# A depthwise convolution spread over four engines and issued a chunk ahead, in a gated-scan kernel

## Chip, cores and metric

One core of one Trainium2 chip; all data is fp32. The metric is device microseconds of one execution. The engines are called PE (TensorE, matmuls), DVE (VectorE), ACT (ScalarE) and POOL (GpSimd); PEld is PE's weight load. SBUF and PSUM are the two on-chip memories.

## The reference, cut to what matters

For each of 4 images of 128 channels and 96x96 pixels, in four scan directions:

```python
t = grouped_1x1(groupnorm(x), in_proj_w, in_proj_b)      # 128 -> 512 channels
u, gate = t[:, :256], t[:, 256:]
u = depthwise_conv(silu(u), dw_w)                        # 5 taps along the scan order
s = ssm_in_w @ u                                         # 32 channels, like a, bb, cc
a = DMIN + (DMAX - DMIN) * sigmoid(ssm_delta_w @ u + ssm_delta_b)
bb, cc = tanh(ssm_b_w @ u + ssm_b_b), tanh(ssm_c_w @ u + ssm_c_b)
h = a * h_prev + bb * s                                  # the scan, along 9216 pixels
u = u + ssm_out_w @ (cc * h + ssm_d * s)
y = out_proj(mix(u * sigmoid(gate)))                     # then fused over the directions
out = x + fuse_w @ y
```

## The kernel before

A *phase* is one image in one pixel order; silu(in_proj(x)) lies whole in SBUF (`sil`), and two *passes*, one for each direction, read it. There are 16 passes. A pass has 18 chunks of 480 pixels and two of 288 (19.3 full ones). In a second pass the front part of the next phase (in_proj and silu) runs too. The 256 channels are two halves of 128. The parts that the change touches:

```python
    def front(ph, c):                      # groupnorm and silu(in_proj) of one chunk
        nc.vector.tensor_scalar(xn, xn, norm[:, 0:1], norm[:, 1:2], ALU.subtract, ALU.mult)
        ...                                # two matmuls pts[j] = w_in . xn, then for each half j
            nc.scalar.activation(sg[:, :n], pts[j][:, :n], AF.Sigmoid, bias=b_in[:, j : j + 1])
            nc.vector.scalar_tensor_tensor(sil[...], pts[j][:, :n], b_in[...], sg[:, :n], ALU.add, ALU.mult)

    def conv_and_gate(st):
        for k, w in taps:                  # half 0: five matmuls with diagonal weights, in PSUM
            nc.tensor.matmul(pu[:, :n], diag[:, w, :], sil[:, 0, bass.ds(o + k, n)], start=..., stop=...)
        for k, w in taps:                  # half 1: one tap on ACT, four on DVE
            if k == 0:
                nc.scalar.activation(u[:, 1, :n], src, AF.Copy, scale=coef)
            else:
                nc.vector.scalar_tensor_tensor(u[:, 1, :n], src, coef, u[:, 1, :n], ALU.mult, ALU.add)
        nc.scalar.copy(u[:, 0, :n], pu[:, :n])
        ...                                # gates: two matmuls pg[j], two sigmoids into gv

    def scan(st):
        ...                                # pp = w_proj . u; tanh, sigmoid, tanh on 32 rows each
        ...                                # POOL: a scaled and clipped; DVE: b*s, scan, c*h, + d*s -> z

    def ssm_out(st):
        ...                                # pu += w_so . z (half 0); pz = w_so . z (half 1)
        nc.vector.tensor_mul(gv[:, 0, :n], pu[:, :n], gv[:, 0, :n])
        nc.vector.tensor_add(u[:, 1, :n], pz[:, :n], u[:, 1, :n])
        nc.vector.tensor_mul(gv[:, 1, :n], u[:, 1, :n], gv[:, 1, :n])

    for n, st in enumerate(steps):         # steps: all chunks of all passes
        conv_and_gate(st)
        if prev is not None:
            ssm_out(prev)
        ...                                # front() of the next phase in second passes
        scan(st)
        if prev is not None:
            accumulate(prev)               # py = w_fin . gv (PE), acc += py (DVE)
        prev = st
```

The instructions are not issued quite in this order: a scheduler in the build reorders them, engine by engine.

## Time and profile before

| | before |
|---|---|
| median of 4 runs, us (range) | 3689.91 (3685.10 to 3701.43) |
| PE / DVE / ACT / POOL busy | 96% / 80% / 43% / 11% |
| mean granted PE clock | 0.938 |
| a full chunk, first pass / second pass | 10.5 us / 11.4 and 12.5 us |
| time at half clock, from the trace's clock records | 455 of 3636 us |

The granted clock of PE over the span, in tenths:

```profile
PEclk8899999999999999999999999999999999999999
```

A 9 is 90% or more.

### The profile page before, as it was taken

To read this page: it belongs to the slowest core of one execution; us is meant where nothing else is said; L and a number is where in the kernel's file an instruction comes from. 1 tells how busy PE (TensorE), PEld (TensorE's weight loads), DVE (VectorE), ACT (ScalarE), POOL (GpSimd) and SP (SyncE) were. 2 spreads that over 40 slices of the span, in tenths; PEclk is the share of its full clock that TensorE was granted. 3 is DMA by queue.
4 is the path that set the end of the run, shared out by engine and by line. 5 is a ranking of instruction groups with operands and counts; after the bars stand their busy time and mean duration, and the time that the engine had idled before them with its cause. 6 is when DMAs were issued, how large, how long until landed. Compare 5 with 4: busy or idle time off the path is not lost.

```text
span 3681.5 us, 27637 instructions
## 1 busy us (share of the span) xinstructions
PE 3543.3 (96%) x9032; PEld 1550.5 (42%) x9032; DVE 2937.6 (80%) x4442; ACT 1572.0 (43%) x2572; POOL 393.2 (11%) x653
## 2 busy tenths in 40 slices
PE   7999999999999999999999999999999999999999
PEld 3334444444443444444443444444444344444444
DVE  7788887788877888778887788777887778877777
ACT  3334444444443444444443444444444444444443
POOL 0011111111111111111111011111111111111111
PEclk8899999999999999999999999999999999999999
DMA  4210000002100000001210000000121000000000
GB/s 145 82 37 12 19 22 0 0 30 65 59 3 0 17 19 17 0 0 46 65 45 0 0 20 22 11 0 3 59 62 32 0 4 21 22 6 0 3 24 25
DMA packets 56625, 92.14 MB, mean 25 GB/s; under 512 B 7296, under 2 KB 56352, under 8 KB 56480
## 3 DMA queue, kind: packets, MB, share of 16 engines
q1 hardware_dynamic: 54720, 89.68, 8.0%
q8 instruction: 70, 1.15, 0.1%
q10 hardware_dynamic: 1760, 0.70, 0.1%
q14 instruction: 75, 0.61, 0.1%
HBM read 71.48 MB, written 18.87 MB: 25 GB/s over the span
## 4 chain that ended last, share of the span: by engine, by line
DVE 46%; PE 41%; issue 6%; ACT 4%; DMA 2%; POOL 0%; ACTq 0%; DVEq 0%; POOLq 0%
DVE u L262 12%; PE pp L288 8%; PE pc L325 8%; PE pc L249 8%; DVE h L309 8%; PE py L340 6%; PE pz L329 6%; DVE z L319 5%; DVE tb L303 4%; DVE z L318 4%; DVE gv L332 3%; PE pu L225 3%; DVE u L331 3%; DVE sil L232 3%; ACT u L260 2%
## 5 line engine op out<-in xcount | busy, mean ns | idle before, releaser
L249 PE MATMUL pc<-sil,diag 128*128 128x480 f32 (+1 forms) x3200 | 1299.5, 552 | 0.0
L262 DVE SCALAR_TENSOR_TENSOR u<-sil,w_dw,u 128x480 f32<-128x480 f32 (+1 forms) x1280 | 889.0, 695 | 135.4 <-ACT u L260 124.0
L249 PEld LDWEIGHTS pc<-sil,diag 128*128 128x128 f32 x3200 | 610.7, 191 | 643.3 <-issue 624.7
L288 PE MATMUL pp<-u,w_proj 128*128 128x480 f32 (+1 forms) x1280 | 705.2, 680 | 3.1 <-DVE u L262 2.0
L265 ACT COPY u<-pc 128x480 f32<-128x480 f32 (+1 forms) x320 | 173.8, 543 | 1074.9 <-PE pc L249 1074.8
L340 PE MATMUL py<-gv,w_fin 128*128 128x480 f32 (+1 forms) x1280 | 614.2, 605 | 0.9
L301 POOL TENSOR_SCALAR a<-a 32x480 f32<-32x480 f32 (+1 forms) x320 | 189.8, 593 | 3252.3 <-ACT a L295 3252.3
L330 DVE TENSOR_TENSOR gv<-pc,gv 128x480 f32<-128x480 f32 (+1 forms) x320 | 203.8, 637 | 343.5 <-PE pc L325 337.1
L275 ACT ACTIVATE gv<-pg,b_in 128x480 f32<-128x480 f32 (+1 forms) x640 | 379.2, 642 | 143.8 <-PE pg L271 133.4
L325 PE MATMUL pc<-z,w_so 32*128 32x480 f32 (+1 forms) x640 | 332.6, 599 | 101.8 <-DVE z L319 100.5
L340 PEld LDWEIGHTS py<-gv,w_fin 128*128 128x128 f32 x1280 | 282.6, 222 | 331.4 <-issue 234.6
L288 PEld LDWEIGHTS pp<-u,w_proj 128*128 128x128 f32 x1280 | 244.3, 212 | 390.2 <-issue 273.8
L260 ACT ACTIVATE u<-sil,w_dw 128x480 f32<-128x480 f32 (+1 forms) x320 | 216.8, 678 | 404.7 <-DVE gv L332 398.0
L309 DVE TENSOR_TENSOR_SCAN h<-a,h,tb 32x480 f32<-32x480 f32 (+1 forms) x304 | 354.7, 1167 | 1.1
L271 PE MATMUL pg<-xn,w_in 32*128 32x480 f32 (+1 forms) x1280 | 345.5, 600 | 0.6 <-ACT gv L275 0.6
L229 ACT ACTIVATE sg<-pu,b_in 128x480 f32<-128x480 f32 (+1 forms) x320 | 201.7, 638 | 274.8 <-PE pu L225 274.7
L329 PE MATMUL pz<-z,w_so 32*128 32x480 f32 (+1 forms) x640 | 301.1, 550 | 0.0
L225 PE MATMUL pu<-xn,w_in 32*128 32x480 f32 (+1 forms) x640 | 264.2, 632 | 9.1 <-DVE sil L232 7.7
L293 ACT ACTIVATE tb<-pp,b_proj 32x480 f32<-32x480 f32 (+1 forms) x320 | 204.0, 637 | 150.8 <-PE pp L288 145.1
L303 DVE TENSOR_TENSOR tb<-pp,tb 32x480 f32<-32x480 f32 (+1 forms) x320 | 198.9, 621 | 70.3 <-ACT z L299 67.3
L232 DVE SCALAR_TENSOR_TENSOR sil<-pu,b_in,sg 128x480 f32<-128x480 f32 (+1 forms) x320 | 219.0, 691 | 24.9 <-ACT sg L229 23.5
L331 DVE TENSOR_TENSOR u<-pz,u 128x480 f32<-128x480 f32 (+1 forms) x320 | 203.9, 637 | 43.7 <-PE pz L329 2.6
(54 smaller groups left out, 2122.3 us busy)
## 6 DMA issues: line engine op xcount, KB each, us to landing
xn<-in_xv SPq DMA_DIRECT2D x72, 240.0 KB, 2.6
acc<-in_xh SPq DMA_DIRECT2D x72, 240.0 KB, 2.8
xn<-in_xh SPq DMA_DIRECT2D x72, 240.0 KB, 2.6
out<-res SPq DMA_DIRECT2D x72, 240.0 KB, 2.0
xs<-in_xh SPq DMA_DIRECT2D x54, 240.0 KB, 2.6
xn<-in_xv SPq DMA_DIRECT2D x8, 144.0 KB, 2.4
acc<-in_xh SPq DMA_DIRECT2D x8, 144.0 KB, 2.4
xn<-in_xh SPq DMA_DIRECT2D x8, 144.0 KB, 2.1
```

The costliest lines, as they stand in the source:

```text
L225: nc.tensor.matmul(pt[:, :n], w_in[q, :], xn[q, span(c)], start=True, stop=True)
L232: nc.vector.scalar_tensor_tensor(sil[:, j, bass.ds(PAD + STARTS[c] * WW, n)], pts[j][:, :n], b_in[:, j : j + 1], sg[:, :n], ALU.add, ALU.mult,
L249: nc.tensor.matmul(pu[:, :n], diag[:, w, :], sil[:, 0, bass.ds(o + k, n)], start=(k == 0), stop=(k == K - 1),)
L262: nc.vector.scalar_tensor_tensor(u[:, 1, :n], src, coef, u[:, 1, :n], ALU.mult, ALU.add)
L271: nc.tensor.matmul(pg[:, :n], w_in[q, :], xn[q, span(c)], start=True, stop=True)
L275: nc.scalar.activation(gv[:, j, :n], pgs[j][:, :n], AF.Sigmoid, bias=b_in[:, 2 + j : 3 + j])
L288: nc.tensor.matmul(pp[:, :n], w_proj[:, j, :], u[:, j, :n], start=(j == 1), stop=(j == 0))
L303: nc.vector.tensor_mul(tb[:, :n], s, tb[:, :n])
L309: nc.vector.tensor_tensor_scan(dirn(h), dirn(a), dirn(tb), 0.0 if st["first"] else carry[0], ALU.mult, ALU.add,)
L325: nc.tensor.matmul(pu[:, :n], w_so[:, 0:P], z[:, :n], start=False, stop=True, skip_group_check=True)
L329: nc.tensor.matmul(pz[:, :n], w_so[:, P:HID], z[:, :n], start=True, stop=True)
L340: nc.tensor.matmul(py[:, :n], w_fin[:, d, j, :], gv[:, j, :n], start=(j == 0), stop=(j == 1))
```

## The change

The intent: PE is the bound, so the convolution is taken off it. Half 0 keeps two taps on PE, and DVE adds three. Half 1 moves to ACT (five scaled copies) and POOL (four adds). It is issued a chunk ahead of its use. Sigmoids become tanh(x/2) with their factors folded into weights; silu is one ACT function; groupnorm is folded into `w_in` and the biases, once an image; the last two DVE steps work on both halves at once, 960 columns.

```diff
+PE_TAPS = (1, 2)
 ...
     def front(ph, c):
-        nc.vector.tensor_scalar(xn[:, span(c)], ...)              # groupnorm
-            nc.scalar.activation(sg[:, :n], ..., AF.Sigmoid, ...)
-            nc.vector.scalar_tensor_tensor(sil[...], ...)
+            nc.scalar.activation(sil[...], pts[j][:, :n], AF.Silu, bias=bn[:, j : j + 1])
 ...
+    def conv(st):
+        u = wk.tile([P, 2, CW], F32, tag="u", bufs=3, name=f"u_{id_}")
+        for k in range(K):                                        # half 1: ACT and POOL
+            src, coef, _ = tap(1, k)
+            t = u[:, 1, :n]
+            if k:
+                t = wk.tile([P, CW], F32, tag="tmp", bufs=3, name=f"tmp_{id_}_{k}")[:, :n]
+            nc.scalar.activation(t, src, AF.Copy, scale=coef)
+            if k:
+                nc.gpsimd.tensor_add(u[:, 1, :n], u[:, 1, :n], t)
+        for i, k in enumerate(PE_TAPS):                           # half 0: PE, then DVE
+            nc.tensor.matmul(pu[:, :n], diag[:, w, :], src, start=..., stop=...)
+        part = pu[:, :n]
+        for k in range(K):
+            if k not in PE_TAPS:
+                nc.vector.scalar_tensor_tensor(u[:, 0, :n], src, coef, part, ALU.mult, ALU.add)
+                part = u[:, 0, :n]
 ...
     def scan(st):                      # one tanh on 96 rows for three calls on 32
+        nc.scalar.activation(t[: 3 * MH, :n], pp[: 3 * MH, :n], AF.Tanh, bias=b_proj[:, 0:1])
+        nc.vector.tensor_mul(bs[qa, :n], s, t[qb, :n])            # then scan, z as before
 ...
     def ssm_out(st):
+        nc.vector.tensor_add(pz[:, :, :n], pz[:, :, :n], u[:, :, :n])
+        nc.vector.scalar_tensor_tensor(gv[:, :, :n], gv[:, :, :n], 1.0, pz[:, :, :n], ALU.add, ALU.mult)
 ...
+    conv(steps[0])
     for n, st in enumerate(steps):
+        scan(st)
+        gates(st)
         if prev is not None:
             ssm_out(prev)
         ...                            # front() of the next phase
+        if n + 1 < len(steps):
+            conv(steps[n + 1])
         if prev is not None:
             accumulate(prev)
```

## The prediction

> **What bounds the kernel now.** I read the page's busy table, then timelines of a steady stretch of each kind of pass, then the groups of instructions with shapes kept apart, then how long POOL's instructions took.
>
> ```profile
> PE 3543.3 (96%) x9032; PEld 1550.5 (42%) x9032; DVE 2937.6 (80%) x4442; ACT 1572.0 (43%) x2572; POOL 393.2 (11%) x653
> ```
>
> PE is busy 96% of the span, DVE 80%, POOL hardly at all. Busy PE alone proves little, so this is PE's timeline over one chunk of a first pass (start, us, count at the right):
>
> ```profile
> 1500.27 1.88 PE L288 MATMUL pp<-u,w_proj 128*128 128x480 f32 x4
> 1501.98 1.77 PE L340 MATMUL py<-gv,w_fin 128*128 128x480 f32 x4
> 1503.59 4.19 PE L249 MATMUL pc<-sil,diag 128*128 128x480 f32 x10
> 1507.71 1.07 PE L271 MATMUL pg<-xn,w_in 32*128 32x480 f32 x4
> 1508.96 1.07 PE L325 MATMUL pc<-z,w_so 32*128 32x480 f32 x2 [0.18 <-DVE z L319]
> 1509.87 0.96 PE L329 MATMUL pz<-z,w_so 32*128 32x480 f32 x2
> 1510.77 0.67 PE L288 MATMUL pp<-u,w_proj 128*128 128x480 f32 x1
> ```
>
> The chunk takes 1510.77 - 1500.27 = 10.50 us. A matmul is two instructions, each 0.41 us from start to start (4.12 us for the ten of the convolution). The two gate matmuls, on different rows of the array, run side by side: four instructions in about 0.85 us. Streaming is 22 x 0.41 + 0.85 = 9.9 us of the 10.5; the rest is a wait for z. So **PE's rate** bounds a first pass. In a second pass the front part of the next phase adds two more matmuls and three DVE operations; there the start of L330 goes from 1740.96 to 1752.40 to 1764.95, so 11.4 and 12.5 us a chunk, the longer one with a projection (pp) that took 3.3 instead of 1.7 us. The windows view gives a granted clock of 0.97 in the first pass 569 to 781 and 0.93 in the second pass 781 to 1012. Of the convolution, PE does 5 of 5 taps for half the channels, 4.1 us of every chunk: the largest single item of the bound.
>
> The durations that I use for the new kernel stand in these groups (count, then busy, mean ns):
>
> ```profile
> L262 DVE SCALAR_TENSOR_TENSOR u<-sil,w_dw,u 128x480 f32<-128x480 f32 x1152 | 822.9, 715 | 129.9 <-ACT u L260 120.0
> L309 DVE TENSOR_TENSOR_SCAN h<-a,h,tb 32x480 f32<-32x480 f32 x280 | 335.6, 1198 | 0.7
> L319 DVE SCALAR_TENSOR_TENSOR z<-pp,d_sb,z 32x480 f32<-32x480 f32 x288 | 203.0, 705 | 9.7
> L331 DVE TENSOR_TENSOR u<-pz,u 128x480 f32<-128x480 f32 x288 | 189.3, 657 | 42.0 <-PE pz L329 1.5
> L303 DVE TENSOR_TENSOR tb<-pp,tb 32x480 f32<-32x480 f32 x288 | 184.8, 642 | 62.4 <-ACT z L299 59.8 <-PE py L340 2.5
> L318 DVE TENSOR_TENSOR z<-z,h 32x480 f32<-32x480 f32 x288 | 184.4, 640 | 0.8
> L345 DVE TENSOR_TENSOR acc<-py,acc 128x480 f32<-128x480 f32 x144 | 152.7, 1061 | 37.3 <-PE py L340 37.3
> ```
>
> Last, DVE and POOL already disturb each other. These are the two engines at one place:
>
> ```profile
> 2327.98 1.83 DVE L262 SCALAR_TENSOR_TENSOR u<-sil,w_dw,u 128x480 f32<-128x480 f32 x2
> ...
> 2328.72 0.58 POOL L301 TENSOR_SCALAR a<-a 32x480 f32<-32x480 f32 x1 [10.45 <-ACT a L295]
> 2329.38 0.86 POOL L302 TENSOR_SCALAR a<-a 32x480 f32<-32x480 f32 x1
> ```
>
> Two convolution taps on DVE took 1.83 us where two elsewhere take 1.46, and the second POOL operation took 0.86 where its median is 0.58.
>
> [...] The trace has eight loads of 1.28 us in all, around the square root. [...]
>
> **The change, part by part, for a full chunk (480 columns).**
> PE: the convolution goes from ten instructions to four, -6 x 0.41 = -2.5 us. Nothing else of PE changes in number. A first pass needs 9.9 - 2.5 = 7.4 us, a second pass 8.2 us (another 0.85).
> ACT: five tap scalings in place of one (0.69 us for the first, then one every 0.60: 3.1 us), one tanh on 96 rows for three on 32 (0.66 for 2.0), gates 1.21, no PSUM copy: 5.0 us; in a second pass two silu add 1.25, so 6.2 us. Not a bound.
> POOL: four adds of 128x480 with two inputs. [...]
> DVE: three taps 3 x 0.715 = 2.15; bs 0.64; scan 1.20; z product 0.64; z sum 0.70; [...] accumulate 1.06 in V order, 0.68 in H order, mean 0.87; statistics in 60 of 320 chunks, 0.1. Sum 8.7 us of durations. In the timeline neighbours without dependence start 0.08 us before the end of the one before, so occupancy is about 8.4. The front part no longer needs DVE (normalising 0.52, two silu products 1.42: 1.9 us saved in every second pass).
> So with no interference DVE is the bound at 8.4 us, above PE at 7.4 to 8.2.
>
> **Interference.** Four DVE operations a chunk have two SBUF inputs: scan, z product, and two of the three taps (the first reads PSUM): 1.20 + 0.64 + 1.43 = 3.3 us. [...] 8.4 + 1.3 = 9.7; I take 9.7 us a chunk, in both kinds of pass.
>
> **The sum.** There are 16 passes of 18 full and two short chunks, 19.3 full ones each. Before, first passes take 212 us for 10.5 x 19.3 = 203, so 9 us at the pass's ends and in slow-clock chunks; I keep 7. The head is 36 us to the first front part, as before; the 20 front parts of the first phase then took some 75 us in front of or between the first chunks, now about 20 x 1.25 = 25 (ACT). Tail 8. 36 + 25 + 8 + 16 x (19.3 x 9.7 + 7) = 69 + 16 x 194 = 3176. The pass-end and front terms partly overlap with work that the scheduler can pull in, so I round down to **3150 us**, 15% under 3689.
>
> **Rivals.** (a) *DVE at its own rate, waits hidden*: if POOL's adds fall in DVE's PSUM operations (5 us of them a chunk), the chunk is 8.5 to 9.0 us and the time 2800 to 2950. For it: the order of DVE's instructions in the trace is not the text's order, taps are already pulled into gaps. [...] (b) *A latency loop*: pp waits for both halves of u; then tanh 0.66, POOL's two steps 1.3, scan 1.2, two z steps 1.35, outputs 2.4, taps 2.2, pp again 1.9. If each engine ran strictly in the order of the text this ring is 11 us, 12 and more with blocked taps, and the time 3500 to 3800: no gain. [...] Against: the convolution is issued a chunk ahead and u has three buffers, so the taps need not lie in the ring. (c) *PE again*, at a lower clock: 8.2/0.93 = 8.8 us in a second pass; under my 9.7, so it only shows if interference is small. [...]
>
> **Range and chances.** 8.5 us a chunk gives about 2810, 10.7 about 3490; I put the range there. Faster needs under 3615, a chunk of 11.1 us[...]. Faster 0.90, within 2% 0.06, slower 0.04.
>
> **What would show it.** Right: PE's busy share falls to about 80% or less and DVE's rises to 90% or more; [...] taps of the first half show a mean well over 0.715 us; first and second passes alike in length; eight table loads still. Wrong: taps at 0.72 us and DVE idle waiting for ACT or POOL (then b); [...] PE still over 90% (then c).

Some of its numbers need their source. DVE's 8.7 us hold 1.16 us for the output sum over both halves and 1.21 for the gating over both. A straight line through the sizes of the one-half sum in the trace of the kernel before, 657 ns at 480 columns (L331) and 455 at 288, gives the same 1.16 us at 960; the 1.21 is that plus the 0.05 by which L319 (705 ns) is longer than L331. These are estimates from two sizes. A two-input add on POOL occurs nowhere in that trace, so no trace showed its length, and the 1.3 us of interference, which rests on that length, was the author's estimate. That DVE and POOL lengthen each other is in the trace: of DVE's taps at 480 columns (L262) the 334 that overlap a POOL step on a take 751 ns on average, the 818 others 700; the POOL steps take 663 ns beside a tap or a z product (347) and 580 elsewhere (229).

## The result, and the profile after

The changed kernel is **slower by 15.8%**: 4274.43 us median of 4 runs (4272.09 to 4277.90) beside 3689.91. Both give the right result. The ratio is 1.1575, with a 95% interval of 1.1553 to 1.1597. A ratio here is the mean time of one kernel's runs over that of the other's runs of the same rounds, so not quite the ratio of the medians.

First the page's busy line and clock row of the changed kernel:

```profile
PE 3665.2 (86%) x7120; PEld 1333.0 (31%) x7120; DVE 3018.6 (71%) x3340; ACT 1801.6 (42%) x2895; POOL 2089.5 (49%) x1936
...
PEclk9887878877878787777787788777778788886777
```

No engine is near its rate. The remarkable thing is PE: it has 21% fewer matmuls than before (7120 for 9032) and is busy *longer* (3665 for 3543 us). The clock row says why: it stands at 7 and 8. By the clock records in the trace PE ran 1791 of 4156 us at half clock, where it was 455 of 3636 before.

The groups of instructions, shapes apart (count, then busy us and mean ns, then the idle time of that engine just before them and what ended it):

```profile
L275 POOL TENSOR_TENSOR u<-u,tmp 128x480 f32<-128x480 f32 x1152 | 1581.8, 1373 | 1054.1 <-ACT u L273 933.1 <-ACT tmp L273 51.7
...
L291 DVE SCALAR_TENSOR_TENSOR u<-sil,w_dw,u 128x480 f32<-128x480 f32 x576 | 568.5, 987 | 11.6
...
L365 DVE TENSOR_TENSOR pz<-pz,u 128x960 f32<-128x960 f32 x288 | 335.6, 1165 | 214.7 <-PE pz L362 198.9 <-PE pu L247 13.0
L366 DVE SCALAR_TENSOR_TENSOR gv<-gv,pz 128x960 f32<-128x960 f32 x288 | 332.2, 1154 | 8.7
L353 DVE TENSOR_TENSOR t<-t,h 32x480 f32<-32x480 f32 x288 | 322.5, 1120 | 9.2
```

The taps with two SBUF inputs take 987 ns on average where the same form took 715 before, and the z product (L353) 1120 where it was 640. Both are blocked by POOL's adds: at 480 columns the 325 of these taps that overlap an add take 1199 ns on average, the other 251 take 713; the 207 z products beside an add 1303, the other 81 652. The tap with a PSUM input takes 714 and 713 (worked out from the trace's records). The two double-width operations cost 1165 and 1154 ns, near the estimates of 1.16 and 1.21 us. So durations are about as foreseen; the idle time is not. The waits, longest first, show it:

```profile
ACT tmp L273 <- POOL u L275: 1127.0, 1090, 2.7
POOL u L275 <- ACT u L273: 1015.4, 303, 8.5
...
PEld pp L324 <- DVE u L291: 490.9, 244, 4.8
ACT u L273 <- DVE pz L365: 483.2, 198, 4.5
DVE bs L337 <- ACT t L329: 459.9, 188, 10.6
...
PE pp L324 <- DVE u L291: 295.1, 166, 4.0
```

ACT waits for POOL, POOL for ACT, ACT for DVE, DVE for ACT. And the projection (pp) waits for the last tap on DVE: its weight load did so 244 times, in 320 chunks, where it waited for a tap 6 times in the kernel before. PE's timeline of one stretch (the bracket at the right is idle time before the instruction and what ended it):

```profile
1482.28 1.07 PE L306 MATMUL pg<-xn,wn 32*128 32x480 f32 x4
1485.72 1.93 PE L362 MATMUL pz<-z,w_so 32*128 32x480 f32 x2 [2.36 <-DVE z L354]
1488.00 3.57 PE L324 MATMUL pp<-u,w_proj 128*128 128x480 f32 x4 [0.34 <-DVE u L291]
```

PE idles 2.4 us, and the projection after it takes 3.57 us instead of the 1.88 that it took in the kernel before. The chain of waits goes on from there to the next projection (start, us, what; t is the z product, gv the gating, u the taps of the next chunk):

```profile
1488.00 3.58 PE pp L324 x4
...
1491.60 0.67 ACT t L329
...
1492.98 1.18 DVE pz L365
...
1494.18 1.22 DVE h L343
...
1495.42 1.16 DVE gv L366
...
1496.61 0.69 DVE t L353
...
1497.33 0.73 DVE u L291
...
1498.07 0.73 DVE z L354
...
1498.83 1.33 DVE u L291
...
1500.18 1.06 DVE acc L381
1501.24 0.64 DVE u L291
...
1501.92 3.28 PE pp L324 x4
```

This turn takes 13.92 us. It is the loop of the prediction's rival (b): projection, tanh, scan, z, outputs and taps one after the other, most of them in DVE's queue, with the projection at half clock (3.58 for 1.9 us) and one tap blocked (1.33 for 0.72). It is one turn of several kinds: others run through POOL's adds. Chunks are irregular: the distance between two scans in one pass runs 11.1, 16.7, 9.8, 17.0. The mean over a pass (the very first left out), divided by 19.3, is 13.2 us a chunk in first passes (255 us) and 14.1 in second passes (272 us), against 11.0 and 12.3 before (212 and 238 us).

### The profile page after: what moved, and what is told of

It reads as the page before. It is cut to its first block, busy times and chain, and to the rows that moved or that the text cites. A ratio compares the mean times of both kernels' runs of the same rounds, so it can differ in the third digit from the quotient of the medians. Undisturbed runs are those within 1.5% of the kernel's fastest.

```text
span 4270.3 us, 25977 instructions
## 1 busy us (share of the span) xinstructions
PE 3665.2 (86%) x7120; PEld 1333.0 (31%) x7120; DVE 3018.6 (71%) x3340; ACT 1801.6 (42%) x2895; POOL 2089.5 (49%) x1936
## 4 chain that ended last, share of the span: by engine, by line
PE 45%; DVE 31%; POOL 17%; ACT 5%; issue 3%; DMA 0%; POOLq 0%; ACTq 0%; DVEq 0%
POOL u L275 13%; PE pp L324 11%; PE pz L362 11%; PE py L376 8%; DVE u L291 8%; PE pc L280 8%; DVE h L343 6%; DVE pz L365 5%; PE pg L306 4%; DVE t L353 3%; PE pu L247 2%; DVE z L354 2%; DVE acc L381 2%; POOL t L334 2%; ACT u L273 2%
## 5 line engine op out<-in xcount | busy, mean ns | idle before, releaser
L275 POOL TENSOR_TENSOR u<-u,tmp 128x480 f32<-128x480 f32 (+1 forms) x1280 | 1700.1, 1328 | 1144.6 <-ACT u L273 1015.4
L273 ACT ACTIVATE tmp<-sil,w_dw 128x480 f32<-128x480 f32 (+1 forms) x1280 | 864.1, 678 | 1127.7 <-POOL u L275 1127.0
L362 PE MATMUL pz<-z,w_so 32*128 32x480 f32 (+1 forms) x1280 | 750.9, 706 | 161.6 <-DVE z L354 161.2
L280 PE MATMUL pc<-sil,diag 128*128 128x480 f32 (+1 forms) x1280 | 783.3, 724 | 7.8 <-DVE u L291 7.7
L343 DVE TENSOR_TENSOR_SCAN h<-t,h,bs 32x480 f32<-32x480 f32 (+1 forms) x304 | 364.1, 1198 | 319.8 <-POOL t L335 314.0
L306 PE MATMUL pg<-xn,wn 32*128 32x480 f32 (+1 forms) x1280 | 564.5, 714 | 17.1 <-ACT gv L310 15.0
L365 DVE TENSOR_TENSOR pz<-pz,u 128x960 f32<-128x960 f32 (+1 forms) x320 | 360.1, 1125 | 239.4 <-PE pz L362 211.8
L310 ACT ACTIVATE gv<-pg,bnorm 128x480 f32<-128x480 f32 (+1 forms) x640 | 376.0, 632 | 53.4 <-PE pg L306 23.6
L366 DVE SCALAR_TENSOR_TENSOR gv<-gv,pz 128x960 f32<-128x960 f32 (+1 forms) x320 | 356.3, 1114 | 9.7
L353 DVE TENSOR_TENSOR t<-t,h 32x480 f32<-32x480 f32 (+1 forms) x320 | 345.9, 1081 | 10.2
```

Of the source, the lines that this page charges most:

```text
L273: nc.scalar.activation(t, src, AF.Copy, scale=coef)
L275: nc.gpsimd.tensor_add(u[:, 1, :n], u[:, 1, :n], t)
L280: nc.tensor.matmul(pu[:, :n], diag[:, w, :], src, start=(i == 0), stop=(i == len(PE_TAPS) - 1),)
L306: nc.tensor.matmul(pg[:, :n], wn[q, :], xn[q, span(c)], start=True, stop=True)
L343: nc.vector.tensor_tensor_scan(dirn(h[qc, :n]), dirn(a), dirn(bs[qa, :n]), 0.0 if st["first"] else carry[0], ALU.mult, ALU.add,)
L353: nc.vector.tensor_mul(t[qc, :n], t[qc, :n], h[qc, :n])
```

## The experiments

Three suspects come out of this reading: the **port** (DVE operations with two SBUF inputs and POOL's adds exclude each other: the taps of 1199 and 713 ns above), the **clock** (PE with less work idles and is given half clock: 1791 us of it for 455), and a **ring** (queues wait for each other in a circle: ACT 1127 us for POOL, POOL 1015 us for ACT). The prediction named them as its interference term and its rivals (c) and (b). The table has all runs; each was also timed against the kernel before on the same chip. "Chunk" is the mean length of first and of second passes, from first scan to first scan, over 19.3; the very first pass, which holds the start, is left out.

| run | what it is | median us | ratio to before, 95% | clock | chunk, us |
|---|---|---|---|---|---|
| after | the changed kernel | 4274 | 1.158 [1.155, 1.160] | 0.79 | 13.2 / 14.1 |
| e1 | convolution of before, rest of the change | 3560 | 0.964 [0.962, 0.966] | 0.98 | 10.9 / 11.4 |
| e2 | port free | 4356 | 1.179 [1.176, 1.181] | 0.77 | 13.5 / 14.3 |
| e3 | PE filled | 4319 | 1.169 [1.167, 1.171] | 0.90 | 14.2 / 13.0 |
| e5 | port free, PE filled | 3976 | 1.078 [1.075, 1.080] | 0.91 | 13.4 / 11.3 |
| e4 | four taps on PE | 3990 | 1.078 [1.074, 1.082] | 0.91 | 12.7 / 12.6 |
| e6 | e4, half of POOL's adds left out | 3715 | 1.007 [1.004, 1.010] | 0.94 | 11.9 / 11.5 |
| e7 | e4, outputs issued before the scan | 4208 | 1.140 [1.137, 1.143] | 0.88 | 13.3 / 13.3 |
| e10 | e4, a fourth buffer for u | 3982 | 1.078 [1.075, 1.080] | 0.92 | 12.6 / 12.5 |
| e9 | e4, convolution behind the tanh | 3901 | 1.056 [1.055, 1.058] | 0.93 | 12.7 / 11.8 |
| e12 | after, convolution behind the tanh | 4325 | 1.171 [1.168, 1.173] | 0.81 | 13.7 / 13.7 |
| e8 | a milder mix of engines | 3780 | 1.024 [1.022, 1.027] | 0.97 | 11.0 / 13.0 |
| e11 | e1, accumulation a chunk later | 3313 | 0.897 [0.895, 0.898] | 0.98 | 9.6 / 11.2 |
| e16 | before, accumulation a chunk later | 3686 | 0.999 [0.997, 1.000] | 0.94 | 11.1 / 12.3 |
| e15 | e8, accumulation a chunk later | 4025 | 1.089 [1.087, 1.092] | 0.89 | 12.3 / 13.4 |
| e13 | after, both of these reorderings | 4267 | 1.156 [1.153, 1.159] | 0.78 | 13.7 / 13.3 |
| e14 | e13, port free | 3656 | 0.990 [0.989, 0.992] | 0.86 | 11.5 / 11.5 |
| e17 | e14, PE filled | 3510 | 0.951 [0.949, 0.953] | 0.98 | 10.8 / 11.3 |
| e18 | e14, four taps on PE, issue in two parts | **3175** | **0.859 [0.857, 0.862]** | 0.98 | 9.6 / 10.3 |

One caution for all of them: each edit lets the build's scheduler order the queues anew, so an edit is never only what its diff says. All results passed the comparison; e6 is wrong on purpose, and the comparison's tolerance does not see it.

### Which part of the change? (e1)

```diff
-        ...   # half 1 on ACT and POOL; half 0 on PE (2 taps) and DVE (3)
+        ...   # half 1: one tap on ACT, four on DVE; half 0: five taps on PE, copied by ACT
```

> The changed kernel with the convolution of before (five taps on TensorE and a copy, one tap on ScalarE, four on VectorE) and all the rest of the change kept. If the spread of the convolution is the cause of the loss (any of my theories about clock, port or ring), the time falls to 3250 to 3550 us, under the kernel before. If the rest (single tanh, products over both halves at once) is to blame, it stays over 3900.

Measured: 3560 us, 10 us above the expected range and 3.6% *faster* than before. So all of the loss, and 714 us more or less, is the spread convolution; silu/tanh, folded groupnorm and double-width products are a gain of 130 us.

### Port and clock, each alone and together (e2, e3, e5)

e2 keeps partial sums of DVE's taps in PSUM, and b*s and h in free rows of the projection's PSUM tile, so that no DVE operation has two SBUF inputs. e3 issues PE's two tap matmuls twice (the second set starts the sum anew), so that PE has 1.6 us more work a chunk and the same result. e5 is both.

```diff
e2:
-                    u[:, 0, :n], src, coef, part, ALU.mult, ALU.add
+                    u[:, 0, :n] if k == K - 1 else part, src, coef, part, ALU.mult, ALU.add
-        nc.vector.tensor_mul(bs[qa, :n], s, t[qb, :n])     # and h: likewise into rows of pp
+        nc.vector.tensor_mul(pp[qa, :n], s, t[qb, :n])
e3:
-        for i, k in enumerate(PE_TAPS):
+        for i, k in list(enumerate(PE_TAPS)) * 2:
```

> The changed kernel with partial sums of the taps, b*s and h kept in PSUM, so that no VectorE instruction has two SBUF inputs; results stay right. Theory port (VectorE and GpSimd exclude each other): taps return to 0.72 us, the z product to 0.65, the GpSimd add to 1.20, and the time falls by 15% or more, to under 3650. Theory clock (TensorE at half speed after idling): the durations fall as well, but the time by under 5%, since TensorE stays idle and slow. Theory ring (in-order queues that wait for one another): 5 to 10%, what the ring's VectorE and GpSimd pieces become shorter.

> The changed kernel with its two tap matmuls of each chunk issued twice (the second time over the first, result unchanged): 1.6 us more TensorE work a chunk and nothing else. Theory clock: granted clock from 0.79 to over 0.9 and the time down by 5% or more. Theories port and ring: time the same or up by up to 1.6 us x 310 = 500 us.

> The edits of the two runs before that each changed nothing (no VectorE instruction with two SBUF inputs; the two tap matmuls issued twice) in one kernel. If port and clock hide each other, so that each shows only with the other gone, the time falls under 3900. Theory ring: the ring seen in the run with four taps on TensorE (u buffer freed, copy, four adds, tanh, two GpSimd steps, scan, z, output sum: 12.4 us) stays and the time is 3950 to 4150, with GpSimd adds at 1.20 and a granted clock near 0.9.

Measured: e2 4356 us, e3 4319 us, e5 3976 us. In e2 the durations went back to normal, so the exclusion is real and the edit took it away:

```profile
L292 DVE SCALAR_TENSOR_TENSOR pc<-sil,w_dw,pc 128x480 f32<-128x480 f32 x576 | 416.3, 723 | 109.4 <-PE pc L280 94.8
...
L336 DVE TENSOR_TENSOR pp<-pp,t 32x480 f32<-32x480 f32 x288 | 194.8, 676 | 812.5 <-ACT t L329 810.3
```

The taps are at 723 ns and POOL's adds at 1200, where they were at 987 and 1373. But the idle time before DVE's b*s grew from 441 us (434.8 of it ended by the tanh) to 812 us, half-clock time rose to 2039 us, and the kernel became 2% *slower* than the changed one. e3 halved the half-clock time (911 us) and gained nothing either; its taps got longer (1082 ns). Only e5 gains 7%, all of it in second passes (14.1 to 11.3 us a chunk); first passes stay at 13.4. Every theory on record for e2 had a gain, and the clock's 5% for e3 did not come. e5 missed the 3900 us that were to show port and clock hiding each other and fell in the range of the ring. So that each hides behind the other is a reading that fits, not one that is shown, and after both something else still holds first passes.

### The first ring (e4, e6, e10, e7)

e4 gives PE four taps, which is useful fill and leaves DVE one tap, with a PSUM input.

```diff
e4:  -PE_TAPS = (1, 2)
     +PE_TAPS = (0, 1, 2, 3)
e6 (on e4, wrong result on purpose):
     -            if k:
     +            if k in (1, 2):
                      nc.gpsimd.tensor_add(u[:, 1, :n], u[:, 1, :n], t)
e10 (on e4):  tag="u", bufs=3  ->  tag="u", bufs=4
e7 (on e4):
     +        if prev is not None:
     +            ssm_out(prev)
              scan(st)
              gates(st)
     -        if prev is not None:
     -            ssm_out(prev)
```

> The changed kernel with four of the five taps of the first half on TensorE and one on VectorE: VectorE loses 1.43 us of two-SBUF taps a chunk, TensorE gains 1.6. Theory port: 1.4 to 2 us a chunk less, 3650 to 3850. Theory clock: more TensorE work, clock over 0.88, 3700 to 3900. Theory ring alone (GpSimd adds and buffers are the ring, VectorE's taps are not in it): within 3% of 4274.

> The run with four taps on TensorE, with two of the four GpSimd adds of a chunk left out (wrong result on purpose; the ScalarE copies stay). Theory ring: 2 x 1.26 us less in a ring of 12.4 us, so 2.5 us a chunk, some 780 us: 3200 to 3350, unless TensorE (9 to 10 us a chunk) bounds it first. If the adds lie beside the path, under 2%.

> The run with four taps on TensorE and a fourth buffer for u. Theory ring through the queue: the scheduler only pulls the copies one chunk further forward, again to the edge of the buffers and in front of the tanh, so 12.5 us a chunk stays: within 2% of 3990. If the shortage of the buffer itself is the cause: 3300 to 3600.

> The run with four taps on TensorE, with the output products of the chunk before issued in front of the scan instead of after it; no work added or removed. Theory ring: the buffer of u comes free before the scan of the next chunk, so scan and z (2.6 us) leave the ring: 9.8 to 11 us a chunk, 3200 to 3600. If the ring is not it, within 3% of 3990.

Measured: e4 3990 us, very even chunks of 12.5 us, though no engine has over some 9.9 us of work (PE in a second pass, by the prediction's sum and two more taps). The chain of waits of e4 in order of time (start, us, what) shows two rings of the same length in turn:

```profile
1798.40 1.18 DVE pz L365
...
1799.61 0.70 ACT u L273
...
1804.28 1.22 POOL u L275
...
1805.52 0.54 ACT tmp L273
...
1806.12 0.65 ACT t L329
...
1808.21 1.22 DVE h L343
...
1810.88 1.18 DVE pz L365
...
1812.09 1.17 DVE gv L366
...
1813.29 1.88 PE py L376 x4
1815.17 1.61 PE pp L324 x4
...
1823.37 1.18 DVE pz L365
```

From pz to pz it is 12.48 us, then 12.49. In the first turn the output sum (pz) frees a buffer of u; ACT starts a convolution; POOL adds four times; an ACT copy waits for a free tmp buffer; **and only then comes the tanh of the running chunk**, at 1806.12 (its projection ended at 1806.00, one turn on 1.83 us before the tanh). The order of ACT's instructions in the trace says why: the copies for the next chunk, and three for the one after it, stand in front of this chunk's tanh, and the last of them waited 0.59 us for POOL. So the tanh waits for POOL's adds and for pz of an earlier chunk, and pz waits for the tanh through scan and z. This ring is e4's own, though: there the tanh starts over 0.3 us after its projection has ended in 203 of 320 chunks, in the changed kernel in 27 (worked out from the trace's records). The changed kernel's tanh mostly waits for a late projection (532 of its 533 us of waits at 480 columns).

e6 bears out that the adds are on e4's path: with two of the four gone the kernel is 275 us faster than e4, though POOL was busy only 47% of e4's span. But 2.4 us out of the ring in every chunk should have given some 780 us; it missed its range of 3200 to 3350 us, and what holds the rest is open. e10 gives the ring another buffer and changes nothing (3982): in the trace the copies stand one more chunk ahead, at the edge of the buffers again. e7 was a miss: it should have shortened the ring and made it longer (4208 us). Its POOL waits 1773 us for ACT's u copies, which wait 1284 us for pz; the z product has a mean of 1403 ns. In 300 of 320 chunks an add stands between the two steps on a in POOL's queue (in e4 in none, in the changed kernel in 130).

### The order of ACT's queue (e9, e12)

The convolution's instructions are held behind the tanh of the running chunk.

```diff
-        nc.scalar.activation(                               # the tanh
+        st["tanh"] = nc.scalar.activation(
 ...
-            conv(steps[n + 1])
+            with tc.issue_after(st["tanh"].ins):
+                conv(steps[n + 1])
```

> The run with four taps on TensorE; ScalarE's part of the convolution of the next chunk is made to queue behind the tanh of this chunk (an order on one engine, no wait for it to finish), so that no copy that waits for a buffer stands in front of a tanh. Same work, same buffers. Theory ring through ScalarE's queue: 12.5 us a chunk falls to what remains, tanh 0.7, copy 0.6, gates 1.2, copy 0.7, adds 5.05, pp 1.1 = 9.4, with VectorE at about the same: 9.8 to 10.8 us, 3200 to 3550. If the order of the queue is not it: within 3% of 3990.

> The changed kernel with nothing but the order on ScalarE of the run with four taps. Port and clock are still there: taps and z product still slowed, clock still under 0.9. Theory ring as the larger part: 3700 to 3950. If port and clock are the larger part: over 4100.

Measured: e9 3901 us, 2% under e4; e12 4325 us, 1% above the changed kernel. Both missed: 2% is what e9's text called a sign that the order is not it, and over 4100 us is what e12's called port and clock as the larger part. The first ring is gone from e9's chain, and two things take its place. The adds now run while DVE scans, so the z product is blocked (mean 1449 ns). And the ring of the second turn above is left: scan, z, pz, gv, py, pp, tanh, a on POOL, scan. It closes because the accumulation's matmul (py) stands in front of the next projection (pp) in PE's queue and waits for gv.

### The second ring (e11, e16)

e11 takes e1, the convolution of before, and runs the accumulation a chunk later; e16 does the same to the kernel before (and opens the pool of work tiles after the set-up, as the changed kernel does).

```diff
-        if prev is not None:
-            accumulate(prev)
-        prev = st
+        if prev2 is not None:
+            accumulate(prev2)
+        prev2, prev = prev, st
 # and gv with bufs=3
```

> A version meant to beat both: the convolution of before with the rest of the change, and each chunk's accumulation one chunk later (three buffers for the gates), so that its matmul no longer stands in front of the next projection and waits for the gating. The 10.7 us a chunk of the run with the convolution of before closes through gating 1.17 and that matmul 1.9; without them TensorE's streaming (9.9 us, 10.7 in second passes) bounds it: 3350 to 3480. If the accumulation is not in the ring: within 2% of 3560.

> The kernel before with the accumulation one chunk later (three gate buffers), nothing else. Theory: the kernel before is bound by PE's rate at 10.5 us in first passes and hardly by the ring, so the time falls little: 3550 to 3690 us. Rival (the late accumulation is what makes the 3313 us, whatever else of the change is there): 3400 us or less.

PE's timeline in e1, a first pass:

```profile
1502.24 4.29 PE L278 MATMUL pc<-sil,diag 128*128 128x480 f32 x10
1507.72 1.88 PE L363 MATMUL py<-gv,w_fin 128*128 128x480 f32 x4 [1.19 <-DVE gv L353]
```

and in e11:

```profile
1507.55 4.29 PE L278 MATMUL pc<-sil,diag 128*128 128x480 f32 x10
1511.68 1.77 PE L363 MATMUL py<-gv,w_fin 128*128 128x480 f32 x4
```

The wait of 1.19 us for gv is gone; the chunk went from 10.7 to 9.3 us, PE is 98% busy, and the time from 3560 to 3313 us, under its range. On the kernel before, which had no such wait, the same edit does nothing (3686 us, ratio 0.999). So the late accumulation is no gain by itself: it removes a wait that the kernel before did not have.

### Other mixes (e8, e15)

Half 0 has four taps on PE and one on DVE; half 1 has one tap on ACT, one on ACT and POOL, three on DVE. e15 adds the late accumulation.

```diff
-PE_TAPS = (1, 2)
+PE_TAPS = (0, 1, 2, 3)
+POOL_TAPS = (1,)
 ...
+            elif k in POOL_TAPS:
+                nc.scalar.activation(t, src, AF.Copy, scale=coef)
+                nc.gpsimd.tensor_add(u[:, 1, :n], u[:, 1, :n], t)
+            else:
+                nc.vector.scalar_tensor_tensor(u[:, 1, :n], src, coef, u[:, 1, :n], ALU.mult, ALU.add)
```

> A version meant to beat both: first half four taps on TensorE and one on VectorE (which reads PSUM, so no copy), second half one tap on ScalarE, one on ScalarE and GpSimd, three on VectorE; the rest of the change kept. TensorE 9.1 to 9.9 us a chunk, VectorE 9.3. Theory ring: only one add in the ring instead of four, 3.8 us less than 12.4, so TensorE and VectorE bound it: 3150 to 3400.

> Half 0: four taps on PE and one on DVE; half 1: one tap on ACT, one on ACT and POOL, three on DVE; accumulation one chunk later. PE has 9.1 us of work in a first pass. Theory: the second ring, which made the same mix 10.7 us a chunk without the late accumulation, is gone, so first passes take about 9.3 us, second passes 10.5 to 11.5; 3250 to 3450 us, near the 3313 us of the late version with the old convolution. Rival (DVE and its waits for POOL bound the mix): 10.5 us or more in first passes, 3600 us or more.

Measured: 3780 and 4025 us. Both missed, e8 by 380 us. e15 is a lesson on orders: in its chain of waits the convolution's first ACT copy waits for the output sum just before it (pz, ACT copy, one POOL add, four DVE taps, pp, tanh, a, scan, z, pz: 12.9 to 14.4 us in its chain of waits, the longer turn with a projection at half clock). e8 had this ring too, at 14.3 us in second passes. In first passes its DVE mostly took pz in front of z's last step (149 chunks); in e15 it comes behind it (123 chunks), so the ring holds these too. One ring was opened and another closed; that the moved accumulation caused it is not shown.

### All causes together (e13, e14, e17, e18)

e13 puts both reorderings on the changed kernel. e14 frees the port too. e17 fills PE too. e18 is e14 with four taps on PE in place of the fill, and the convolution issued in two parts:

```diff
e18, on e14:
-PE_TAPS = (1, 2)
+PE_TAPS = (0, 1, 2, 3)
 ...
+        if n + 1 < len(steps):
+            conv(steps[n + 1], (0,))       # half 0: PE and one DVE tap, before this chunk's scan
         scan(st)
         gates(st)
 ...
             with tc.issue_after(st["tanh"].ins):
-                conv(steps[n + 1])
+                conv(steps[n + 1], (1,))   # half 1: ACT and POOL
```

> The changed kernel with both rings opened: the convolution of the next chunk is issued behind this chunk's tanh, and the accumulation runs one chunk later, with three gate buffers. Theory (the slowness is the two latency rings; the engines' own work would fit): a chunk of 10 to 11.3 us, 3300 to 3650 us, granted clock above 0.9. Rival (the DVE/POOL exclusion, 4 x 1.2 + 1.2 us of POOL and 3.3 us of DVE's two-SBUF-input operations[...], or PE at half clock while it idles, is enough by itself): above 3900 us, with the z product and the taps still long and the clock under 0.85.

> As the run before, and in addition no DVE operation has two SBUF inputs, so nothing of DVE can be blocked by POOL. Rings opened, port free; PE still has only two taps. Theory: DVE's sum with unblocked durations, 8.4 to 9.5 us a chunk, 2850 to 3250 us, under the 3313 us of the best version so far. Rival (the granted clock falls by half when PE has 7.4 us of work in a chunk, which takes the gain back): pp near 3.3 us, clock under 0.85, and 3500 us or more.

> The run with the port freed and both rings opened (3656 us, where chunks of 8.1 us at full clock alternate with chunks of 15.5 us at half clock), with the two tap matmuls issued twice, so that PE has 9.1 us of work a chunk in a first pass and 9.9 in a second. Nothing of DVE, ACT and POOL changes. Theory (the half clock alone is what holds it): half-clock time under 500 us, chunks of 9.2 to 10.2 us, 3100 to 3350 us, although PE does more work. Rival (another ring through DVE's queue is left): a chunk of 11 us or more at full clock, 3600 us or more.

> Port free, accumulation one chunk later, four taps of half 0 on PE, and the convolution issued in two parts: half 0 (PE and one DVE tap) ahead of this chunk's scan, half 1 (ACT and POOL) behind this chunk's tanh. PE has 9.1 and 9.9 us of work a chunk, as in the run beside it, but all of it useful. The ring that is left runs tanh 0.66, a on POOL 1.2, four adds 4.8, pp 1.7, so 8.4 us and about 9 with hand-overs. Theory: the spread convolution is then bound by PE's rate, 9.3 to 10.3 us a chunk, 3150 to 3400 us, near the 3313 us of the best version or under it. Rival (POOL's five adds in the ring plus waits make it longer): 11 us a chunk, 3600 us or more.

**e13** fell to its rival: 4267 us, nothing gained. So the two rings that e4 and e9 showed are not by themselves what costs the changed kernel its time. With the adds beside the scan, its scan has a mean of 1592 ns, its z product 1379 and POOL's adds 1430. **e14**, the same with the port free, is 3656 us: 14% less, where freeing the port alone (e2) had cost 2%. POOL's order is the same in both (two steps on a, then four adds); PE's and DVE's differ in part, so a share of the 14% may be order. e14 too missed its range of 2850 to 3250 us. Its rival, the half clock, is in PE's timeline:

```profile
2006.55 1.88 PE L324 MATMUL pp<-u,w_proj 128*128 128x480 f32 x4
...
2014.69 2.84 PE L324 MATMUL pp<-u,w_proj 128*128 128x480 f32 x4
...
2020.95 3.57 PE L280 MATMUL pc<-sil,diag 128*128 128x480 f32 x4
...
2030.17 1.88 PE L324 MATMUL pp<-u,w_proj 128*128 128x480 f32 x4
```

From projection to projection it is 8.1 us at full clock, and 15.5 us where the clock is halved. **e17** does 1.6 us *more* PE work in every chunk and is 4% faster than e14 (3510 us): half-clock time fell from 1020 to 160 us. It missed its range of 3100 to 3350 us, though: a third ring (last DVE tap, pp, tanh, b*s, scan, z, and the next chunk's taps behind them in DVE's queue) holds it at 9.9 to 10.6 us in first passes and 11.1 in second ones. Its members are those of the turn shown for the changed kernel: this ring was there from the start. In every run with two taps on PE the projection's weight load waits for a DVE tap, 110 to 579 us in all; in e4, with four, 9 us. **e18** opens it and lands in its expected range: 3175 us, 14.1% under the kernel before. Its page, and the timelines of PE, ACT and POOL in a first pass:

```profile
PE 3008.7 (95%) x8400; PEld 1287.7 (41%) x8400; DVE 2227.1 (70%) x2700; ACT 1678.5 (53%) x2895; POOL 1856.5 (58%) x1936
...
PEclk9999999999999999999999999999999999999998
```

```profile
1703.29 1.07 PE L325 MATMUL pp<-u,w_proj 128*128 128x480 f32 x2 [0.55 <-POOL u L276]
...
1707.82 3.38 PE L283 MATMUL pc<-sil,diag 128*128 128x480 f32 x8
...
1712.58 1.07 PE L325 MATMUL pp<-u,w_proj 128*128 128x480 f32 x2 [0.56 <-POOL u L276]
```

```profile
1704.40 0.66 ACT L330 ACTIVATE t<-pp,b_proj 96x480 f32<-96x480 f32 x1 [4.28 <-PE pp L325]
...
1706.63 1.86 ACT L274 ACTIVATE tmp<-sil,w_dw 128x480 f32<-128x480 f32 x3
```

```profile
1707.46 5.07 POOL L276 TENSOR_TENSOR u<-u,tmp 128x480 f32<-128x480 f32 x4 [0.99 <-POOL t L336]
```

The chunk is 9.29 us, PE waits 0.56 us of it for POOL's last add and works the rest. So a first pass is still held by a ring, if a tight one: projection, tanh, in ACT's queue behind it a copy, two gates and the first copy into tmp, then four adds, and the projection again. (The bracket names POOL's step on a, which had ended 1 us before; the first copy had only just ended, by its start and a length of about 0.7 us.) In a second pass PE works without a wait, 10.1 us a chunk. e18 is 4% faster than e11, the best version with the old convolution (from different rounds, each against the kernel before). What each of e18's three edits is worth by itself was not run; nor was e18 with the port left as it was.

## Why the prediction was wrong

- **PE's work, 7.4 and 8.2 us a chunk.** The count was right: the matmuls fell to 7120, and e14's full-clock chunks of 8.1 us leave no room for more. That this would free time was wrong; see the clock.
- **ACT, DVE and POOL durations.** Nearly right. The double-width sum was put at 1.16 and measured 1165 ns; the gating at 1.21 and 1154 ns; a tap with a PSUM input at 0.715 and 714 ns. Why the gating took no longer than the sum, where L319 took 48 ns more than L331 before, was not tested. POOL's add, which no trace had shown, takes 1.20 us at 480 columns and 0.795 at 288 with the port free (e2), which makes about 2.1 ns a column and 0.19 us fixed, an estimate from these two sizes. The table loads were not "eight still" but eleven of 1283 ns, where the kernel before had eight: about 4 us in all.
- **Interference, 1.3 us of DVE waits a chunk.** Right in size: twice 987 less 723 ns, and 1120 less 647 ns for the z product (the free values from e2 and e5), is 1.0 us. In both, whose DVE operations have one SBUF input at most, the taps take 723 ns beside the same adds.
- **"8.4 + 1.3 = 9.7; I take 9.7 us a chunk, in both kinds of pass": this step failed.** It adds up the busiest engine and its blockages as if the queues kept that engine fed. Measured: 13.2 and 14.1 us a chunk, with DVE idle 29% of the span.
- **The step under it failed first: rival (b) was dismissed because "the convolution is issued a chunk ahead and u has three buffers, so the taps need not lie in the ring".** They did lie in it. In the changed kernel the projection waited for DVE's last tap in most chunks (244 waits of its weight load, 491 us; 295 us of PE itself), and the turn shown above runs projection, tanh, outputs, scan, z, taps, projection: 13.9 us where (b) added up 11. The next chunk's taps were issued ahead, but in DVE's one queue they came between and behind this chunk's scan and z. With four taps on PE and one on DVE (e4) that wait is gone (9 us), but there another ring holds. Buffers did not help where they were tried: with e10's fourth one the copies only moved further forward. Rival (b) gave "the time 3500 to 3800"; the changed kernel is worse than that.
- **Rival (c) failed too.** It took the clock as that of the kernel before, 0.93, "so it only shows if interference is small". The clock went with PE's work: 0.77 to 0.86 in the five runs with two taps on PE and no fill, 0.88 to 0.98 in every other. It is not the work alone: e8 and e15 do the same work at 0.97 and 0.89. By the clock records 195 of the changed kernel's 196 half-clock stretches are 3.41 us long or a multiple of it (99 of 100 in the kernel before). In the 3.41 us before such a stretch the changed kernel's PE was busy a median 48% of the time, with a longest gap of 2.5 us in the median, where a full-clock 3.41 us followed by more full clock has a median of 100%. In the kernel before, the same medians are 86% and 0.5 us, and no gap was over 3.1 us; in e14 (176 stretches) PE was busy a median 70% and no gap was over 3.41 us (worked out from the matmul and clock records after the first 300 us; the ends of matmuls are modelled). How much idling brings the half clock on is not shown. So a PE that waits works slower in these runs (the projection took 3.58 us for 1.88), which lengthens the rings through it, as in the turn above; that this idles it further is argued, not shown.
- **What was called wrong in advance.** "Taps at 0.72 us and DVE idle waiting for ACT or POOL (then b)". DVE did wait for ACT, but the taps were long as well: both mechanisms were there, and the list had no line for that. Of the signs of being right, PE fell to 86% busy and not to 80, and DVE fell to 71% where 90 was forecast.
- **Where the prediction would have been right.** The predicted time, 3150 us, is what a spread convolution takes once port, clock and rings are dealt with together (e18: 3175 us). That is luck and no proof of its sum: e18 has four taps on PE, and its chunks of 9.3 and 10.1 us are set by a ring through POOL and by PE, with DVE busy 70%.

What is shown: the loss lies in the spread convolution (e1). None of the port (e2), the clock (e3) and the two rings of e4 and e9 (e13) explains it alone; taking any one away changed the time by -0.2 to +2%. Taken away in turn, rings and port give 14%, the clock another 4%, the last ring and the more useful PE taps another 10%. What stays open is how much of 4274 us belongs to each, since the order in which they are removed decides what each seems to be worth, and every edit also moved the queues. The ring through the taps was not opened alone in the changed kernel.

## What to carry to other kernels

Before adding up engine times, write down each engine's queue for one chunk in issue order and look for circles: here an early issue of the next chunk's work did not help where this chunk's critical path stood behind it (the turns of 13.9 us in the changed kernel and 12.5 us in e4). If taking work from PE leaves it idle for part of each chunk, look at its granted clock (0.79 in the changed kernel, 1791 of 4156 us at half clock), and try giving it useful work back rather than freeing it: 1.6 us more a chunk took e14's 1020 us at half clock to 160 in e17. And when a single fix does nothing, try fixes in pairs before dropping the theory: here two that each cost 1 to 2% gained 7% together, and the port, worth nothing alone, was worth up to 14% once two rings were open.
